# Seven quarter products for A11 B11 in the block pairs of six matrices, and another place for the last rows of one, in a relational graph layer on one core

## The chip, the core and the metric

The kernel runs on one core of a Trainium2 chip. The core has five engines with queues of their own: TensorE (matmuls, PE), VectorE (DVE), ScalarE (ACT), GpSimd (POOL) and SyncE (SP, which here only starts transfers). Each engine works through its queue in order, and engines wait for each other on semaphores. The metric is the device time of one launch in microseconds, lower is better. Given is the median of several executions, and besides one execution that was profiled.

## The reference, cut to what matters

```python
h = jnp.maximum(_layernorm(x, axis=-1), 0.0)          # x: 1250 x 1024
# u: root term, bias, and for 8 edge types the mean of the neighbours times a matrix
out = h @ root + bias
for r in range(8):
    mask = (edge_type == r).astype(h.dtype)
    sums = segment_sum(h[src] * mask[:, None], dst, num_segments=n)
    cnt = segment_sum(mask, dst, num_segments=n)
    out = out + (sums / jnp.maximum(cnt, 1.0)[:, None]) @ weight[r]
u = out
z = jnp.concatenate([u, h], axis=1) @ w_gate + b_gate
y = x + jnp.tanh(u) * z + h * (1.0 - z)
```

All is float32. There are 20000 edges, eight 1024 x 1024 matrices `weight[r]`, one `root`, and `w_gate` of 2048 x 1024.

## The kernel before, in words

The kernel multiplies first and gathers afterwards. It forms h times each matrix of the list `mats`: matrices zero to seven are `weight[0..7]`, eight is `root`, nine is the lower half of `w_gate` (for h), and ten is the upper half (for u). Products with the weights are stored to DRAM tables `y`. For each node GpSimd gathers the rows of `y` that belong to its incoming edges, and VectorE adds them to the node's row with a weight (L1170, here called a gather add). Gathers run beside the products of matrices five to nine. Matrix ten is the last stage, in which the gate is applied (L1496 on).

**Products of quarters.** The 1250 rows are ten blocks of 128. A step (s, i) takes matrix s with blocks i and i + 5 together, i from 0 to 4. The two row blocks and the matrix are cut into quarters (A11 to A22, B11 to B22; a B quarter is 512 x 512), and `product` (L341) forms the result with seven products in place of eight, by the Strassen-Winograd scheme. The sums of A quarters (S1 to S4) lie ready in `h_op[i]`; those of B quarters (t1 to t4) are made by VectorE for each matrix (`make_t1` to `make_t4`, L167 to L181). A product is four matmuls of 512 columns into one PSUM bank, and `product` runs them in the order A11 B11, S1 t1, S2 t2, then S4 B22, S3 t3, A12 B21 and A22 t4 (by the names of the code the first, fifth, sixth, third, seventh, second and fourth). TensorE adds up in PSUM; after some products ScalarE copies the bank out and VectorE adds other parts in SBUF. The bank `b` is a chain: A11 B11 is copied out as one result, then S2 t2 is added to the same bank, and so on.

**Pairs.** In matrices one to nine, steps 0 and 1, and steps 2 and 3, are pairs (`paired`, L446); step 4 stands alone. In a pair the product A12 B21 of both blocks is formed together, by seven smaller products over quarters of quarters (class `Second`, L183). From matrix four on (`thirds`, L450) S4 B22 is treated likewise (class `Third`, L254). Each small product is two matmuls of 256 columns (`Second.add`, L212), and needs sums that VectorE forms: `Second.right` and `left` (L201, L206), `Third.sums` and `next_sums` (L267, L273). Their tiles are the spare factor buffers `f.spare` and four tiles `room` (`inner0` to `inner3`). The pieces are slipped into the order of `product` by the dictionary `fill`, under the names of the products.

**What sets the order.** The program is scheduled by hand (`manual_schedule`, L54): each engine gets its instructions in the order in which the Python code emits them. After each product `done()` calls `between(j)`, j from 0 to 6; `step` uses it (`beside`, L477) to emit the loads of the next matrix, the sums for factors, and lastly one or two gather adds (`spread`, L1223). Where a sum of quarters is needed depends on TensorE's order, and where it stands in VectorE's queue on the `between` call that emitted it. In step 4 the factors of the next matrix are made (`make_t1` at j = 1, `make_t2` at 4, `make_t3` at 5), `make_t4` and the `right` and `left` sums at j = 0 of the next matrix's step 0.

**Memory.** Products take PSUM banks from `bank()`, six buffers named `ps`. Two more banks, `ps_n` and `ps_q`, hold the edge sorting's matmuls early on and two of `Third`'s sums later. A result row is a tile of the pool `rows` (four buffers, L102), stored by SP (`put`, L465).

Of the kernel before, what the change touches and what calls it, by code (L numbers as in the profile page):

```python
# [19 lines left out]
def tile_rgcn_highway(  # L20
# [98 lines left out]
    node_dram = [dram.tile([KEYS, 1], I32, name=f"node_dram{g}") for g in range(G)]  # L119

    def bank():
        return psum.tile([P, 512], F32, name="ps", bufs=6)


    wbuf = [wpool.tile([P, KQ, Q], F32, name=f"w{i}") for i in range(9)]
# [128 lines left out]
    class Third:  # L254
# [53 lines left out]
        def last_to(self, to, to1, c):  # L308
# [3 lines left out]
                                 to1.rearrange("p (a n) -> p a n", a=2),  # L312
                                 self.b[:, None, :].to_broadcast([P, 2, H]))

    def transposed(aop, part, of, n, relu=False):


        for half, to in enumerate(((A11, A12), (A21, A22))[part]):
            p = bank().rearrange("p (k f) -> p k f", k=KQ)
            for i in range(KQ):  # L320
                k = KQ * half + i
                nc.tensor.transpose(p[:, i, :n], of[:n, k * P:(k + 1) * P], ident[:n, :n])  # L322
            to_n, p_n = aop[:, to, :, :n], p[:, :, :n]
            if half and relu:
                nc.vector.tensor_scalar_max(to_n, p_n, 0.0)
            elif half:
                nc.vector.tensor_copy(to_n, p_n)
            else:
                nc.scalar.activation(to_n, p_n, AF.Relu if relu else AF.Copy)
            if n < P:  # L330
                nc.gpsimd.memset(aop[:, to, :, n:], 0.0)
# [7 lines left out]
                                                                     aop[:, b])  # L339

    def product(aop, w, to, between=lambda j: None, last=None, pieces=1, whole=True,  # L341
                fill=None, second=None, third=None, inner=None):

        c11, c12 = to[0][:, :Q], to[0][:, Q:]  # L350
        c21, c22 = to[1][:, :Q], to[1][:, Q:]
        step = [0]

        def add(b, i, fresh=False, at=slice(0, Q)):
            for k in range(KQ):
                nc.tensor.matmul(b[:, at], aop[:, i, k, :], w.of[i][:, k, at],  # L356
                                 start=(fresh and k == 0), stop=(k == KQ - 1),
                                 skip_group_check=True)

        def done():  # L360
            between(step[0])
            step[0] += 1

        def filled(name):
            if fill and name in fill and fill[name]():
                done()

        def p3():
            add(c, S4)
            if third:  # L370
                third(c)
            else:
                nc.vector.tensor_add(c12, c12, c)  # L373
            done()
            filled("third")

        def p7():
            d = rows.tile([P, Q], F32, name="part", bufs=2)
            add(b, S3)
            nc.scalar.copy(d, b)  # L380
            nc.vector.tensor_add(c22, c22, d)  # L381
            done()
            filled("seventh")
            return d

        def p2():
            a = bank()
            add(a, A12, True)
            nc.vector.tensor_add(c11, c11, a)
            done()  # L390

        b = bank()
        c = inner.hold() if inner and inner.holds else bank()
        add(b, A11, True)
        nc.scalar.copy(c11, b)  # L395
        done()
        filled("first")
        if second:
            second()
            p2()  # L400
        add(c, S1, True)
        nc.scalar.copy(c22, c)  # L402
        done()
        filled("fifth")
        add(b, S2)
        nc.scalar.copy(c12, b)  # L406
        done()
        filled("sixth")
        if whole and not third:
            p3()  # L410
            d = p7()
            if not second:
                p2()
        else:
            d = p7()
            if third:
                last(d, 0)
            if inner:
                inner.then(c)
                done()  # L420
                filled("third")
            else:
                p3()
        if pieces == 1:
            add(b, A22)
            if last:
                last(b, 0)
            else:
                nc.scalar.copy(c21, b)  # L429
        else:  # L430
            for j in reversed(range(pieces)):
                at = slice(j * Q // pieces, (j + 1) * Q // pieces)
                b = bank()
                add(b, A22, True, at)
                last(b[:, at], at.start, d[:, at])
        done()
        filled("fourth")
# [12 lines left out]
    def thirds(s):  # L450

        return s > EARLY

    waiting, waiting_third = {}, {}

    def step(s, i, between=lambda j: None, second=None):

        two = paired(s, i)
        t = [rows.tile([P, D], F32, name="row") for _ in range(2)]
        if two and i == 2:  # L460
            t.reverse()
        if two and i % 2 == 0:
# [12 lines left out]
            nc.sync.dma_start(to, t[:n])  # L475

        def beside(j):  # L477
            new = fac[s + 1]
            if i == 0 and j == 0 and s > 0:
                fac[s].make_t4()  # L480
            if two and i == 0:
                sums(j)
            if q and i % 2 == 0 and j == 1:
                q.sums()
            if q and i % 2 and j == 1:
                q.next_sums()
                q.first_to(to[:, Q:])
            if q and i % 2 and j == 4:
                q.fifth_to(t[0][:, Q:])
            if two and (i, j) == (1, 6):  # L490
                Second(fac[s], 2).left()
            if (s, i, j) == (0, 0, 3) or (s > 0 and (i, j) == (3, 0)):
                new.load_first()
            if (s, i, j) == (0, 0, 3) or (s > 0 and (i, j) == (3, 2)):
                new.load_next()
            if i == NP - 1:
                if j == 0:
                    new.load_b22()
                elif j == 1:
                    new.make_t1()  # L500
                elif j == 3:
                    new.load_b21()
                elif j == 4:
                    new.make_t2()
                elif j == 5:
                    new.make_t3()
            between(j)

        def sums(j):
# [5 lines left out]
            if j == (0 if s > EARLY else 4):  # L515
                e.left()

        fill = {}
        q = None
        if two:  # L520
            e, to = waiting[i - i % 2]
            if thirds(s):
                if i % 2 == 0:
                    waiting_third[i] = Third(fac[s], i, room)
                q = waiting_third[i - i % 2]
                q.holds = i % 2 == 0

                def then(c):
                    if q.holds:
                        q.second(c)  # L530
                    else:
                        q.last(c)
                        q.last_to(to[:, Q:], t[0][:, Q:], c)
                        put(i - 1, 0, to)

                q.then = then
            if i == 0:
                fill = dict(sixth=lambda: (e.second(), e.second_to_first(to)))
            elif i == 1:
                fill = dict(first=lambda: (e.first(), q and q.first(), 0)[-1],  # L540
                            fifth=lambda: (e.sixth(), True),
                            sixth=lambda: (e.seventh(), e.to_first(to), 0)[-1],
                            seventh=lambda: (e.fourth(), e.to_second(t[0]),
                                             q or put(i - 1, 0, to), 0)[-1],
                            third=lambda: (e.fourth_to_second(t[0]), 0)[-1])
            elif i == 2:
                fill = dict(sixth=lambda: e.first(),
                            seventh=lambda: e.sixth(),
                            third=lambda: (e.seventh(), e.to_first(to), 0)[-1],
                            fourth=lambda: (e.fourth(), True))  # L550
            else:
                fill = dict(first=lambda: (e.to_second(t[0]), e.fourth_to_second(t[0]),
                                           q and q.first(), 0)[-1],
                            sixth=lambda: (e.second(), True),
                            seventh=lambda: (e.second_to_first(to), q or put(i - 1, 0, to),
                                             0)[-1])
        product(h_op[i], fac[s], t, between=beside, whole=not two, fill=fill, second=second,
                inner=q)
        for part in range(2):
            if part or not two or i % 2:  # L560
                put(i, part, t[part])
# [578 lines left out]
    with ExitStack() as edges_part:  # L1140
# [4 lines left out]
        inner_pool = edges_part.enter_context(tc.tile_pool(name="inner", bufs=1))  # L1145
        room = [inner_pool.tile([P, 2, n], F32, name=f"inner{k}")
                for k, n in enumerate((H, H, P, P))]

        fresh = [GOT]

# [87 lines left out]
        def passes_needed():  # L1238
# [7 lines left out]
                                             w_of[:, g, d, K[g][d]:], axis=AX.X)  # L1246
            nc.vector.reduce_max(most[:, 1:2], far_k, axis=AX.X)
            for _ in range(30):
                yield
            p = bank()  # L1250
            nc.tensor.transpose(p[:1, :P], most[:, 0:1], ident)
# [327 lines left out]
```

## Time and profile before

| what | value |
|---|---|
| median of 3 runs | 1359.27 us (1354.49 to 1364.49) |
| the profiled execution | 1362.24 us |
| its span, first to last instruction | 1360.2 us |
| granted TensorE clock, mean | 0.996 |
| gather adds (L1170) | 193, 246.9 us on VectorE |
| matrix six (721 to 838 us): VectorE busy | 88.5 of 117 us |
| matrix nine (1079 to 1200 us): VectorE busy | 91.4 of 121 us |
| waits of gather adds for their gather | 86.3 us in 45 |

A group line of the profile reads: line, engine and operation, output<-inputs by the program's names, shapes, count | busy us, mean ns | idle time of the engine before it and what ended most of it. A timeline row reads: start, duration, engine, line, operation, count, and in brackets the idle time before it. An fp32 matmul of the program stands in the trace as two records. L numbers are lines of the kernel before.

### The profile page before, as it was taken

The numbers are of one execution on the slowest core, as the hardware profiler recorded it, in microseconds if no ns is written. First come the engines' busy times: TensorE is split into PE (matmuls) and PEld (weight loads), VectorE is DVE, ScalarE is ACT, GpSimd is POOL, SyncE is SP. The second block draws the span as 40 slices with busy tenths as digits, with TensorE's granted clock in tenths as the row PEclk, the third lists the DMA queues.
The fourth block names the chain that finished last, engine by engine and source line by source line (L and its number), as shares of the span: only waits on it lengthen the run. The fifth ranks groups of instructions, "written<-read, shape, count | busy, mean of one in ns | idle before, by whom it ended". The sixth has DMA issues, their size and how long they took to land.

```text
span 1360.2 us, 13211 instructions
## 1 busy us (share of the span) xinstructions
PE 1343.3 (99%) x3954; PEld 686.7 (50%) x3954; DVE 940.9 (69%) x1929; ACT 370.2 (27%) x816; POOL 583.6 (43%) x510
## 2 busy tenths in 40 slices
PE   9999999999999999999999999999999999989997
PEld 5444455455445545554554555455455455544443
DVE  6855967876785834425767777876867696667875
ACT  3335566465741111111111111111111111122210
POOL 0001655754552456001444564555366356434631
PEclk9999999999999999999999999999999999989999
DMA  8744675854863251144648779788788957879971
GB/s 307 273 184 151 93 141 139 212 85 110 175 167 108 54 156 34 46 155 151 213 126 303 236 240 357 255 284 290 240 274 281 315 178 227 284 263 270 337 202 58
DMA packets 106908, 271.15 MB, mean 199 GB/s; under 512 B 22692, under 2 KB 24946, under 8 KB 106704
## 3 DMA queue, kind: packets, MB, share of 16 engines
q1 hardware_dynamic: 46640, 120.01, 29.5%
q0 software_dynamic: 44064, 118.28, 27.8%
q10 hardware_dynamic: 16128, 31.98, 7.4%
q8 instruction: 31, 0.51, 0.2%
q14 instruction: 45, 0.37, 0.1%
HBM read 212.71 MB, written 75.66 MB: 212 GB/s over the span
## 4 chain that ended last, share of the span: by engine, by line
PE 76%; DMA 10%; issue 8%; POOL 4%; DVE 2%; SPq 0%; ACT 0%; POOLq 0%; DVEq 0%; ACTq 0%
PE ps L356 61%; PE ps L214 8%; DMA got<-y,idx 6%; PE ps_n L356 2%; PE ps_q L214 2%; DMA got<-hr_dram,node 2%; POOL got L1165 1%; PE ps_n L214 1%; DMA w<-in_L_gnn_weight_dram 1%; DVE u L1170 1%; DMA z_dram<-row 1%; POOL got L586 1%; POOL h_op L586 1%; PE ps L322 1%; POOL out_dram L592 1%
## 5 line engine op out<-in xcount | busy, mean ns | idle before, releaser
L356 PE MATMUL ps<-w,h_op 128*128 128x512 f32 x2512 | 1108.1, 594 | 5.4 <-ACT row L402 4.1
L356 PEld LDWEIGHTS ps<-w,h_op 128*128 128x128 f32 x2512 | 472.2, 190 | 548.2 <-issue 529.6
L1165 POOL DMA_INDIRECT got<-y,idx x193 | 247.3, 1281 | 345.3 <-DVE u L1170 212.1
L1170 DVE SCALAR_TENSOR_TENSOR u<-got,w_of,u 128x1024 f32<-128x1024 f32 (+1 forms) x193 | 246.9, 1282 | 88.8 <-DMA got<-y,idx 86.3
L982 POOL DMA_INDIRECT table<-row_col,at_i x157 | 176.5, 1124 | 157.4 <-DVE at_i L978 73.7
L381 DVE TENSOR_TENSOR row<-row,part 128x512 f32<-128x512 f32 x55 | 37.9, 689 | 113.9 <-ACT part L380 113.9
L429 ACT COPY row<-ps 128x512 f32<-128x512 f32 x50 | 29.2, 584 | 215.5 <-PE ps L356 215.5
L380 ACT COPY part<-ps 128x512 f32<-128x512 f32 x55 | 32.2, 585 | 180.4 <-PE ps L356 180.4
L395 ACT COPY row<-ps 128x512 f32<-128x512 f32 x55 | 32.2, 585 | 163.1 <-PE ps L356 157.9
L214 PE MATMUL ps<-w,w 128*128 128x256 f32 x288 | 71.3, 380 | 0.0
L406 ACT COPY row<-ps 128x512 f32<-128x512 f32 x55 | 32.2, 586 | 133.3 <-PE ps L356 133.3
L214 PEld LDWEIGHTS ps<-w,w 128*128 128x128 f32 x288 | 54.4, 190 | 18.3 <-issue 12.4
L402 ACT COPY row<-ps 128x512 f32<-128x512 f32 x43 | 25.1, 585 | 124.7 <-PE ps L356 108.1
L968 DVE SCALAR_TENSOR_TENSOR junk<-k_bc,key_col,before 128x128 f32<-128x128 int32 x157 | 55.0, 350 | 4.2
L908 DVE TENSOR_TENSOR seen<-seen,ps_n 128x100 f32<-128x100 f32 x157 | 40.2, 256 | 24.7 <-PE ps_n L903 20.6
L214 PE MATMUL ps<-w,h_op 128*128 128x256 f32 x216 | 56.0, 382 | 0.0
L373 DVE TENSOR_TENSOR row<-row,ps 128x512 f32<-128x512 f32 x30 | 20.5, 684 | 47.8 <-PE ps L356 32.2
L214 PEld LDWEIGHTS ps<-w,h_op 128*128 128x128 f32 x216 | 40.5, 190 | 25.6 <-issue 22.3
L169 DVE TENSOR_TENSOR w<-w,w 128x2048 f32<-128x2048 f32 (+1 forms) x12 | 25.3, 2112 | 37.1 <-PE ps L356 35.9
L885 ACT ACTIVATE is_lo<-io,less_lo 128x128 bf16<-128x128 f32 x157 | 50.2, 391 | 0.7 <-DMA xh_dram<-xt 0.7
L623 POOL DMA_INDIRECT node_dram<-ids,pos_i x20 | 28.8, 1440 | 41.5 <-issue 41.5
L356 PE MATMUL ps_n<-w,h_op 128*128 128x512 f32 x96 | 43.3, 593 | 1.6 <-DVE row L309 1.6
(216 smaller groups left out, 1180.8 us busy)
## 6 DMA issues: line engine op xcount, KB each, us to landing
y<-row SPq DMA_DIRECT2D x72, 512.0 KB
w<-in_L_gnn_weight_dram ACTq DMA_DIRECT2D x21, 1024.0 KB
w<-in_L_gnn_weight_dram SPq DMA_DIRECT2D x10, 1024.0 KB
k_bc<-keys_dram SPq DMA_DIRECT2D x39, 256.0 KB
l_bc<-los_dram SPq DMA_DIRECT2D x39, 256.0 KB
w<-in_L_gnn_w_gate_dram ACTq DMA_DIRECT2D x6, 1024.0 KB
h_dram<-h_op SPq DMA_DIRECT2D x9, 512.0 KB
u<-in_L_gnn_bias_dram SPq DMA_DIRECT2D x9, 512.0 KB
```

What stands on the lines that cost most here:

```text
L214: nc.tensor.matmul(p, a[:, k, :], b[:, k, :], start=(fresh and k == 0), stop=(k == 1), skip_group_check=True)
L356: nc.tensor.matmul(b[:, at], aop[:, i, k, :], w.of[i][:, k, at], start=(fresh and k == 0), stop=(k == KQ - 1), skip_group_check=True)
L380: nc.scalar.copy(d, b)
L381: nc.vector.tensor_add(c22, c22, d)
L395: nc.scalar.copy(c11, b)
L406: nc.scalar.copy(c12, b)
L885: nc.scalar.activation(is_lo[:, i, :], io, AF.Abs, bias=less_lo[:, c0 + i:c0 + i + 1])
L908: nc.vector.tensor_add(seen[j][:, i, :], was, p[:, i, :])
L968: nc.vector.scalar_tensor_tensor(junk, o["k_bc"][:, i, :], key_col[:, c:c + 1], before, op0=OP.is_equal, op1=OP.mult, accum_out=rank[:, c: ...
L982: ins = nc.gpsimd.indirect_dma_start(out=table[:, :], out_offset=bass.IndirectOffsetOnAxis(ap=at_i[:n, i:i + 1], axis=0), in_=row_col[:n, ...
L1165: nc.gpsimd.indirect_dma_start(out=t[:n], out_offset=None, in_=y[g][:, :], in_offset=bass.IndirectOffsetOnAxis(ap=at[:n, d, k:k + 1], axis=0),
L1170: nc.vector.scalar_tensor_tensor(u[:n], t[:n], w, u[:n], op0=OP.mult, op1=OP.add)
```

## The change

In matrices four to nine A11 B11 of both blocks of a pair takes seven products of quarters too. The class `First` does this. Unlike `Second` and `Third` it forms its results in PSUM alone: ScalarE or VectorE write a partial sum into a bank, and TensorE adds the next product on top. The two results, `to0` and `to1`, are then the banks `b` of the two blocks' chains. The first four small products (`early`) run one step ahead, before that step's last product; the last three (`late`) in the pair's first step, in which S1 t1 now comes first and the third product right after. `First` shares the tiles `room` with `Third`, has one more tile `p5_room`, and its banks are a name of their own, so `ps` has four buffers and `ps_b` two. `fill` and the positions j of some sums are rearranged for this, in odd steps the third product comes before the seventh, and in third blocks `seventh` and `fourth` of `Second` are emitted together. In matrix nine's step 4 the two result rows lie in the S2 and S3 places of `h_op[2]` and `h_op[3]`, not in row buffers. The transposes of `passes_needed` are emitted at j = 4 of a step 4.

```diff
     def bank():
-        return psum.tile([P, 512], F32, name="ps", bufs=6)
+        return psum.tile([P, 512], F32, name="ps", bufs=4)
+    def lead():
+        return psum.tile([P, 512], F32, name="ps_b", bufs=2)
...
+    class First:
+        def __init__(self, f, i, room, p5):
+            b = f.place["b11"]
...
+        def sums(self):
+            Third.sums(self)
+        def next_sums(self):
+            Third.next_sums(self)
+        def early(self):
+            self.to0 = lead()
+            self.x, y = bank()[:, :H], bank()[:, :H]
+            Second.add(self, self.x, self.a11, self.b11, True)
+            nc.scalar.copy(self.to0[:, :H], self.x)
+            Second.add(self, y, self.s1, self.t1, True)
+            nc.scalar.copy(self.p5, y)
+            Second.add(self, self.to0[:, :H], self.a12, self.b21)
+            Second.add(self, self.x, self.s2, self.t2)
+            nc.vector.tensor_add(self.to0[:, H:], self.x, self.p5)
+        def late(self):
+            self.to1 = lead()
+            Second.add(self, self.x, self.s1, self.t1)
+            nc.scalar.copy(self.to1[:, :H], self.x)
+            nc.vector.tensor_add(self.to1[:, H:], self.x, self.p5)
+            Second.add(self, self.to0[:, H:], self.s2, self.b22)
+            Second.add(self, self.to1[:, :H], self.a22, self.t2)
+            return self.to0
...
+        def p1():
+            if first is None:
+                b = lead()
+                add(b, A11, True)
+            else:
+                b = first.late() if inner.holds else first.to1
+            nc.scalar.copy(c11, b)
+            done()
...
+        if first and inner.holds:
+            c = p5()
+            b = p1()
+            inner.then(c)
+            done()
+        else:
+            b = p1()
...
         else:
+            if inner and not inner.holds:
+                inner.then(c)
+                done()
+                filled("third")
             d = p7()
             if third:
                 last(d, 0)
-            if inner:
-                inner.then(c)
-                done()
-                filled("third")
-            else:
+            if not inner:
                 p3()
+        if early:
+            early()
...
+    def next_first(s, i):
+        if thirds(s) and i == 1:
+            return s, 2
+        if thirds(s + 1) and i == NP - 1 and s + 1 < NM - 1:
+            return s + 1, 0
+        return None
...
-        t = [rows.tile([P, D], F32, name="row") for _ in range(2)]
+        if (s, i) == (NM - 2, NP - 1):
+            t = [h_op[k][:, S2:S3 + 1].rearrange("p a k f -> p (a k f)") for k in (2, 3)]
+        else:
+            t = [rows.tile([P, D], F32, name="row") for _ in range(2)]
...
-            if q and i % 2 == 0 and j == 1:
+            if q and i % 2 == 0 and j == 3:
                 q.sums()
...
-            if q and i % 2 and j == 4:
+            if q and i % 2 and j == 3:
                 q.fifth_to(t[0][:, Q:])
+            if coming and j == (4 if i == 1 else 2):
+                first_sums()
...
+        def first_sums():
+            waiting_first[coming] = First(fac[coming[0]], coming[1], room, p5_room)
+            waiting_first[coming].sums()
+        def early():
+            waiting_first[coming].early()
+            waiting_first[coming].next_sums()
...
             elif i == 2:
                 fill = dict(sixth=lambda: e.first(),
                             seventh=lambda: e.sixth(),
-                            third=lambda: (e.seventh(), e.to_first(to), 0)[-1],
                             fourth=lambda: (e.fourth(), True))
+                fill["fourth" if q else "third"] = lambda: (e.seventh(), e.to_first(to), 0)[-1]
+                if q:
+                    fill["fourth"] = lambda: (e.seventh(), e.to_first(to), e.fourth(), True)
...
             for _ in range(30):
                 yield
+            while at_call != [NP - 1, 4]:
+                yield
             p = bank()
```

## The prediction

> **What bounds the kernel now.** I read the busy times first, then what TensorE waits for, then the queue of VectorE around the places that the change touches.
>
> ```profile
> PE 1343.3 (99%) x3954; PEld 686.7 (50%) x3954; DVE 940.9 (69%) x1929; ACT 370.2 (27%) x816; POOL 583.6 (43%) x510
> ...
> PE ps L356 <- ACT row L402: 4.1, 1, 4.1
> PE ps_n L356 <- DVE row L309: 1.6, 1, 1.6
> ```
>
> TensorE is busy all the time, and its longest waits are one of 4.1 us and one of 1.6 us. So time is won only by fewer matmul columns or by those waits, and any new wait of TensorE is paid in full.
>
> ```profile
> 1201.30:1204.70 3.40, 0.44 (x2) 0.00 (x0) 2.16 (x1) 0.00 (x0) 2.67 (x2) 1.00 1.03 416
> 1204.70:1211.60 6.90, 5.78 (x7) 2.53 (x8) 0.00 (x0) 4.36 (x5) 0.00 (x0) 0.51 1.03 420
> ...
> 1205.18 0.58 ACT L402 COPY row<-ps 128x512 f32<-128x512 f32 x1 [9.64 <-DMA z_dram<-row]
> ```
>
> The windows (columns: stretch, sum, PE, PEld, DVE, ACT, POOL, then the granted clock) show the 4.1 us wait in matrix nine's last row block: a copy waits for a row buffer that is still being stored. The clock in the next 6.9 us is half. Work from 1205.8 to 1211.6 runs at half speed and loses another 2.9 us.
>
> ```profile
> 741.91 0.68 DVE L389 TENSOR_TENSOR row<-row,ps 128x512 f32<-128x512 f32 x1
> 742.51 2.28 DVE L177 TENSOR_TENSOR w<-w,w 128x2048 f32<-128x2048 f32 x1
> 744.72 2.60 DVE L1170 SCALAR_TENSOR_TENSOR u<-got,w_of,u 128x1024 f32<-128x1024 f32 x2
> 747.23 2.28 DVE L181 TENSOR_TENSOR w<-w,w 128x2048 f32<-128x2048 f32 x1
> ...
> 753.09 0.42 DVE L210 TENSOR_TENSOR w<-h_op,w 128x256 f32<-128x256 f32 x1
> 753.43 2.60 DVE L1170 SCALAR_TENSOR_TENSOR u<-got,w_of,u 128x1024 f32<-128x1024 f32 x2
> 755.94 0.42 DVE L268 TENSOR_TENSOR inner<-h_op 128x256 f32<-128x256 f32 x1
> ...
> 747.34 3.60 PE L356 MATMUL ps_n<-w,h_op 128*128 128x512 f32 x8
> ```
>
> This is VectorE's timeline from the last block of matrix five into the first of matrix six. Nothing between L389 and L268 has idle time before it: VectorE works off 14 us of queue in a row. L389 itself needs the product A12 B21, which ended at 740.48 (two products of 3.43 us before the ps_n product at 747.34). Today TensorE needs none of that queue soon.
>
> **Removed.** The trace shows an fp32 matmul as two records. Eight records of 512 columns take 3.43 us, start to next start, so 0.429 each; eight of 256 take 1.73, so 0.216:
>
> ```profile
> 802.59 3.60 PE L356 MATMUL ps<-w,h_op 128*128 128x512 f32 x8
> ...
> 806.02 1.89 PE L214 MATMUL ps<-w,w 128*128 128x256 f32 x8
> 807.75 1.03 PE L214 MATMUL ps_n<-w,h_op 128*128 128x256 f32 x4
> ```
>
> A pair's two A11 B11 are 16 records of 512, 6.86 us; the seven quarter products are 28 of 256, 6.05 us. Twelve pairs (matrices four to nine, two each): **-9.8**. Matrix nine's last rows go to old factors, so L402's wait and the slow clock behind it go: 4.1 + 2.9 = **-7.0**. The third product now comes before the seventh, 3.43 us earlier, so the 1.6 us on L309 goes: **-1.6**. Sum -18.4.
>
> **Added, first pairs.** In `late`, TensorE's a22 t4 into `to1[:, :H]` waits for VectorE's add into `to1[:, H:]` (same tile). In the changed program's order that add stands behind: the c11 add of A12 B21 (L389), make_t3 (L177), the gather adds, `early`'s add, four `next_sums`, make_t4 (L181), four `right` (L204), four `left` (L207 to L210) and the gather adds of the step: exactly the queue shown, plus 2.23 us (a quarter add 0.34 pace to pace, sums 1.88 as L268 to L271). TensorE arrives after `early` (16 records, 3.46), A22 (3.43), A11's place taken by S1 (3.43) and two quarter products (1.73): 12.05 us after A12 B21 ended. For matrix six: VectorE is through at 755.94 + 2.23 + 0.42 = 758.6; TensorE is there at 740.48 + 12.05 = 752.5: a wait of 6.1. The same sum from the other timelines, with VectorE's position after the last gather add of the queue (or the last L210) and the end of A12 B21 found as above:
>
> - matrix four: fourteen weight instructions (L609 to L615, 5.1 us) stand there in place of gather adds, and VectorE waits 0.6 for `early`: 520.20 + 2.23 + 0.6 + 0.42 against 505.87 + 12.05: 5.5
> - matrix five, no gathers: 632.30 + 3.25 against 623.06 + 12.05: 0.4
> - seven: 873.13 + 2.65 against 857.66 + 12.05: 6.1
> - eight, one gather add: 987.63 + 2.65 against 974.85 + 12.05: 3.4
> - nine: 1112.49 + 2.65 against 1092.04 + 12.05: 11.1. VectorE comes to L389 7.7 us late there, behind late gathers (5.9 us of waiting before 1088.8).
>
> Together **+32.6**. The first sums (1.9 us) put into the last block ahead of this are hidden: in matrices three to six VectorE waits 1.8 to 3.4 us for L381 after them, in seven and eight for gathers. Without that cover they would lengthen each of these waits by up to 1.9.
>
> **Added, second pairs.** The same wait stands at the third block. VectorE's queue there is shorter: from the third product's end, adds and first sums 3.4, two gather adds 2.6, L248 to L381 1.4, gather add 1.3, quarter adds and `next_sums` 2.6, `left` 1.4, two gather adds 2.6, 0.4: 15.8 us against TensorE's 16.3. Left is the handoff alone: copy and add behind the quarter product (0.62 + 0.5) less 0.86: 0.3 in five matrices. In matrix nine VectorE stands 7.4 us late at L309; I leave 5 of it, since the wait before lets it catch up. **+6.5** (2 to 12).
>
> **Added, third block.** `seventh` and `fourth` of Second now follow each other; the second needs ScalarE's copy of the first.
>
> ```profile
> 800.86 1.03 PE L214 MATMUL ps<-w,h_op 128*128 128x256 f32 x4
> ...
> 801.98 0.37 ACT L220 COPY w<-ps 128x256 f32<-128x256 f32 x1 [0.33 <-PE ps L214]
> ```
>
> TensorE could go on at 801.73, the copy ends at 802.35: 0.65 with the signal, six times: **+3.9** (0 to 4.5).
>
> **Added, the clock.** The row: 4.1 us of waiting halved the clock. Read alone, waits of 5.5, 6.1, 6.1 and 11.1 us all do it, four times 2.9, 11.6. [...]
>
> **At nothing.** 36 quarter copies of ScalarE (0.37 each, 13 us) lie in its 73% idle time; in the chain each is followed by a product of 0.86. VectorE's 120 new instructions (4.45 us a pair, 53 in all) beyond the waits above: it idles 28 of 117 us in matrix six (row below), but in nine it is full, which is a rival. PSUM's six banks become four and two: the banks taken in `early` were last read a product or more before. `sums` of Third moves two products later; L269 ends at 756.96 and is needed at 768.98, so cover remains. On SP the half-row store waits for the adds of one more product; behind it stand the next stores and `load_next`, not due for a block. If that cover were gone, a copy would wait as L402 did, 4 us. POOL issues the same.
>
> **Sum.** -18.4 + 32.6 + 6.5 + 3.9 + 9.3 = +33.9. The profiled run took 1362.2 (span 1360.2), 3 us over the median 1359.3. Carried to the median: **1393.2**.
>
> **Rivals.**
>
> ```profile
> 721.00:838.00 117.00, 117.00 (x329) 61.87 (x328) 88.50 (x105) 19.10 (x37) 59.02 (x50) 1.00 0.81 282
> 1079.00:1200.00 121.00, 118.91 (x332) 62.25 (x331) 91.39 (x108) 18.91 (x37) 66.10 (x50) 1.00 0.75 244
> ```
>
> *Faster:* VectorE reaches the add in `late` before TensorE does. For it: a quarter of VectorE's time is idle. The point is 12.05 us after A12 B21. Against: the queue starts only when that product ends, and takes 9.2 to 20.5 us before anything is added. Then -18.4 + 3.9 + 1.8 (the handoff at six second pairs): about 1347, and 1341 if the copies in the third block are covered too.
> *No change:* the waits come, but the clock stays up and matrix nine's falls to 5, VectorE having caught up: -18.4 + 26.5 + 3 + 3.9 = +15 at most, and a wait or two shorter brings it to 1365 to 1374.
> *Worse:* in matrix nine VectorE is busy 91 of 121 us and waits for gathers in most of the rest, so its 9 us of new work there and in eight isn't absorbed: 5 more at each pair of nine and 3 at the last products: about 1407.
> That the quarters don't replace the whole products is excluded by the program: 96 fewer matmuls of 512 columns, 168 more of 256.
>
> **Chances.** Forecast 0.70, worse 0.08, no change 0.13, faster 0.09. A change of less than about 1% (13.6 us) can't be told from none in this kernel: faster 0.06 (the faster rival's better part), same 0.17, slower 0.77. The unknown costs alone span 1372 to 1412; with part of the rivals on either side the range is 1364 to 1412.
>
> **What would show it.** Right: TensorE waits on VectorE's add in `late`, near 6 us in matrices four, six and seven, little in five, most in nine, and half clock after these; no L402 wait for z_dram; quarter products at 0.216 a record. Wrong: those waits under 2 us, or VectorE reaching `late` early.

## The result, and the profile after

| | before | after |
|---|---|---|
| median of 4 runs | 1356.93 us (1354.49 to 1364.49) | 1406.67 us (1403.78 to 1407.83) |
| the profiled execution | 1362.24 us | 1407.83 us |
| its span | 1360.2 us | 1406.0 us |
| granted TensorE clock, mean | 0.996 | 0.985 |

The ratio is 1.0349, with a 95% interval of 1.031 to 1.0388: slower. The time is 13.5 us above the forecast of 1393.2. Against the medians of this table the loss is 49.7 us, 15.8 more than the 33.9 forecast; the median of before is lower here than the 1359.27 the forecast started from, because a fourth run is in it.

Busy times come first again, from the page of the kernel after:

```profile
PE 1349.1 (96%) x4098; PEld 719.6 (51%) x4098; DVE 995.2 (71%) x2049; ACT 381.9 (27%) x852; POOL 589.3 (42%) x510
```

TensorE has 144 records more and is busy for 5.8 us longer, though it has less to do; the half clock of six stretches (37.6 us at 0.50 in all, TensorE busy in 24.4 of them) is in that number. The span grew by 45.8, so most of the loss is TensorE standing still. The waits of TensorE in the kernel after (engine, what it wrote, its line, what it waited for, the line of that; us in total, times, longest):

```profile
PE ps_b L218 <- DVE ps_b L354: 29.8, 7, 6.7
PE ps_b L400 <- ACT part L424: 8.1, 12, 0.7
PE ps L218 <- ACT w L235: 2.8, 6, 0.5
PE ps_q L1049 <- issue: 1.8, 1, 1.8
PE ps L366 <- DVE row L417: 1.5, 1, 1.5
```

L354 is VectorE's add in `late`, the wait that the forecast is built on. L235 is the copy in the third block, also forecast. The second line was not: L424 is ScalarE's copy of S3 t3 in `p7`. The waits on L402 and L309 of before are gone.

VectorE's timeline into matrix six, the counterpart of the one shown for before (start, duration, engine, line, operation, count):

```profile
759.02 0.67 DVE L433 TENSOR_TENSOR row<-row,ps 128x512 f32<-128x512 f32 x1
759.61 2.27 DVE L181 TENSOR_TENSOR w<-w,w 128x2048 f32<-128x2048 f32 x1
761.82 1.27 DVE L1266 SCALAR_TENSOR_TENSOR u<-got,w_of,u 128x1024 f32<-128x1024 f32 x1
763.01 0.41 DVE L348 TENSOR_TENSOR ps_b<-ps,inner 128x256 f32<-128x256 f32 x1
...
765.22 1.27 DVE L1266 SCALAR_TENSOR_TENSOR u<-got,w_of,u 128x1024 f32<-128x1024 f32 x1
766.41 2.27 DVE L185 TENSOR_TENSOR w<-w,w 128x2048 f32<-128x2048 f32 x1
768.62 0.67 DVE L208 TENSOR_TENSOR w<-w 128x512 f32<-128x512 f32 x1
...
772.26 0.42 DVE L214 TENSOR_TENSOR w<-h_op,w 128x256 f32<-128x256 f32 x1
772.60 2.60 DVE L1266 SCALAR_TENSOR_TENSOR u<-got,w_of,u 128x1024 f32<-128x1024 f32 x2
775.12 0.43 DVE L354 TENSOR_TENSOR ps_b<-ps,inner 128x256 f32<-128x256 f32 x1
```

From L433 (L389 before) to L354 VectorE is never idle: 16 us of queue. make_t4 (L185), the four `right` (L208) and four `left` (L211 to L214) take 766.41 to 772.60, 6.2 us, and nobody needs them before the add. TensorE's timeline over the same time, with the idle time before an instruction and its releaser in brackets, and one line of ScalarE's:

```profile
767.85 1.03 PE L218 MATMUL ps_b<-w,inner 128*128 128x256 f32 x4
775.60 2.07 PE L218 MATMUL ps_b<-inner,h_op 128*128 128x256 f32 x4 [6.72 <-DVE ps_b L354]
...
784.63 3.68 PE L400 MATMUL ps_b<-w,h_op 128*128 128x512 f32 x8
788.98 1.55 PE L400 MATMUL ps_b<-w,h_op 128*128 128x512 f32 x3 [0.68 <-ACT part L424]
```

```profile
788.34 0.59 ACT L424 COPY part<-ps_b 128x512 f32<-128x512 f32 x1 [3.79 <-PE ps_b L400]
```

The first wait is 6.72 us. At 784.63 begin the eight records of S3 t3; A22 t4 goes into the same bank and must wait until ScalarE has copied it out. It begins after 4.35 us in place of 3.43. By single records, from the start of the last one to the next start, less the usual 0.429, such a gap is 0.84 us; there are twelve, two in each of matrices four to nine.

The clock, in windows around that wait (stretch, sum, PE, PEld, DVE, ACT, POOL busy with counts, granted clock, DMA share, GB/s):

```profile
767.85:771.26 3.41, 1.03 (x5) 0.57 (x3) 3.38 (x6) 0.94 (x2) 3.10 (x2) 1.00 0.35 77
771.26:774.68 3.42, 0.00 (x0) 0.00 (x0) 3.35 (x6) 0.00 (x0) 0.76 (x2) 0.50 0.72 264
774.68:778.09 3.41, 2.49 (x6) 2.05 (x7) 3.38 (x5) 0.00 (x0) 2.80 (x3) 0.50 0.21 58
778.09:781.50 3.41, 3.41 (x7) 1.82 (x6) 3.04 (x5) 0.00 (x0) 1.91 (x3) 0.50 0.89 243
781.50:784.92 3.42, 3.42 (x11) 1.82 (x10) 0.03 (x1) 0.59 (x1) 2.04 (x3) 1.00 0.86 320
```

The clock falls to 0.50 while TensorE waits, and stays there for 5.9 us of work (2.49 + 3.41) after the wait has ended.

### The profile page after: what moved, and what is told of

Read it like the earlier page. It is cut to its first block, busy times and chain, and to the rows that moved or that the text cites. A ratio compares the mean times of both kernels' runs of the same rounds, so it can differ in the third digit from the quotient of the medians.

```text
span 1406.0 us, 13671 instructions
## 1 busy us (share of the span) xinstructions
PE 1349.1 (96%) x4098; PEld 719.6 (51%) x4098; DVE 995.2 (71%) x2049; ACT 381.9 (27%) x852; POOL 589.3 (42%) x510
## 5 line engine op out<-in xcount | busy, mean ns | idle before, releaser
L400 PE MATMUL ps_b<-w,h_op 128*128 128x512 f32 x1560 | 705.9, 598 | 9.1 <-ACT part L424 8.1
L400 PEld LDWEIGHTS ps_b<-w,h_op 128*128 128x128 f32 x1560 | 294.4, 191 | 344.1 <-issue 319.4
L1261 POOL DMA_INDIRECT got<-y,idx x193 | 260.7, 1351 | 373.6 <-DVE u L1266 231.5
L400 PE MATMUL ps<-w,h_op 128*128 128x512 f32 (+1 forms) x760 | 338.5, 589 | 0.0
L400 PEld LDWEIGHTS ps<-w,h_op 128*128 128x128 f32 x760 | 143.3, 190 | 163.4 <-issue 160.7
L424 ACT COPY part<-ps_b 128x512 f32<-128x512 f32 x55 | 32.2, 586 | 217.8 <-PE ps_b L400 215.8
L467 ACT COPY row<-ps_b 128x512 f32<-128x512 f32 x54 | 31.7, 586 | 202.3 <-PE ps_b L400 195.9
L492 ACT COPY row<-ps_b 128x512 f32<-128x512 f32 x49 | 28.7, 585 | 187.8 <-PE ps_b L400 186.4
L218 PE MATMUL ps<-w,h_op 128*128 128x256 f32 x264 | 69.0, 384 | 2.8 <-ACT w L235 2.8
L218 PEld LDWEIGHTS ps<-w,h_op 128*128 128x128 f32 x264 | 49.1, 190 | 31.7 <-issue 21.9
L442 ACT COPY row<-ps_b 128x512 f32<-128x512 f32 x54 | 31.7, 587 | 97.1 <-PE ps_b L400 82.6
L450 ACT COPY row<-ps 128x512 f32<-128x512 f32 x42 | 24.6, 586 | 109.3 <-PE ps L400 96.6
L218 PE MATMUL ps<-inner,inner 128*128 128x256 f32 x192 | 49.3, 379 | 0.0
```

The source lines that it names most:

```text
L218: nc.tensor.matmul(p, a[:, k, :], b[:, k, :], start=(fresh and k == 0), stop=(k == 1), skip_group_check=True)
L1261: nc.gpsimd.indirect_dma_start(out=t[:n], out_offset=None, in_=y[g][:, :], in_offset=bass.IndirectOffsetOnAxis(ap=at[:n, d, k:k + 1], axis=0),
```

## The experiments

Each experiment has a short name, given with its result. The ratios are to the kernel before, measured on the same chip in the same session; times from different sessions are compared through them. "The first wait" is that of a matrix's first pair on L354, as excess over the usual pace from start to start. In the kernel after it is 5.9, 0.6, 6.9, 6.3, 2.7 and 6.6 us in matrices four to nine, 28.9 in all.

**Theory A: the wait is the order of VectorE's queue. Rival: VectorE has too much work, in whatever order.** The edit moves what nobody needs yet behind the add:

```diff
-            if i == 0 and j == 0 and s > 0:
+            if i == 0 and s > 0 and j == (1 if s > EARLY else 0):
                 fac[s].make_t4()
...
-            for k in range(4) if s > EARLY and j == 0 else (j,) if s <= EARLY and j < 4 else ():
+            for k in range(4) if s > EARLY and j == 1 else (j,) if s <= EARLY and j < 4 else ():
                 e.right(k)
-            if j == (0 if s > EARLY else 4):
+            if j == (1 if s > EARLY else 4):
                 e.left()
```

> The changed kernel with make_t4 and the right and left sums of a step 0 emitted after its third call of done() position (j = 1) and no longer at j = 0, from matrix four on, so that VectorE's add in late stands ahead of them. Theory A (the wait is the order of VectorE's queue): these instructions are 2.25 + 8 x 0.5 = 6.3 us of the queue ahead of the add. TensorE's excess at the first pair falls from 5.9, 0.6, 6.9, 6.3, 2.7 and 6.6 us to 0.3 to 0.7 each, 28.9 to about 3.6 in all, and the half clock behind them (10.7 us of excess) goes: 1406.7 - 25 - 10.7 = about 1371 us. Rival B (VectorE has too much work beside matrices six to nine, whatever its order): the waits move to the sums that were put back (L211 to L214, L218 on w) or to L354 in the second pair; 1395 or more.

Measured (both_moved): 1376.52 us, ratio 1.0097 (1.0066 to 1.0129). Its longest waits:

```profile
PE ps_b L400 <- ACT part L424: 8.1, 12, 0.7
PE ps_b L218 <- DVE ps_b L354: 7.5, 5, 2.5
PE ps_q L1049 <- ACT s_b L1033: 3.6, 2, 2.3
PE ps L366 <- DVE row L417: 3.3, 1, 3.3
PE ps L218 <- ACT w L235: 2.8, 6, 0.5
```

and VectorE at the same place of matrix six:

```profile
757.56 3.91 DVE L1266 SCALAR_TENSOR_TENSOR u<-got,w_of,u 128x1024 f32<-128x1024 f32 x3
761.39 0.42 DVE L354 TENSOR_TENSOR ps_b<-ps,inner 128x256 f32<-128x256 f32 x1
761.72 2.28 DVE L185 TENSOR_TENSOR w<-w,w 128x2048 f32<-128x2048 f32 x1
```

Where L185 stood in front of L354 it now stands behind it, and the first waits are 0.8 in six, 1.5 in nine and under 0.3 elsewhere. The mean granted clock of both_moved's profiled execution is 0.997, against 0.985 in the kernel after. A good 2.5% of the time, some 34 of the 49.7 us, is this order with the half clock behind it. Not all is: the *second* pairs of six, eight and nine now wait 1.7, 1.7 and 2.7 us on L354, where VectorE runs through 20 to 26 us of queue without a gap. So the rival holds in part, for these. Each of those three queues begins with a gather add that had waited 1.0 to 5.1 us for its gather, so late gathers may have a part in it. The one of six:

```profile
786.20 1.28 DVE L1266 SCALAR_TENSOR_TENSOR u<-got,w_of,u 128x1024 f32<-128x1024 f32 x1 [5.11 <-DMA got<-y,idx]
```

The dose: `right` and `left` moved alone, make_t4 left where it was.

> The changed kernel with only the eight right and left sums emitted at j = 1 in place of j = 0; make_t4 stays ahead of the add in late. Theory A (queue order): each first wait that is longer than that falls by the 8 x 0.5 = 4.05 us taken from the queue: matrix four 5.9 to 1.9, six 6.9 to 2.8, seven 6.3 to 2.2, nine 6.6 to 2.6, five and eight to 0.3 to 0.7; about 10.5 us in all in place of 28.9. The clock: stalls of 2 to 3 us are under the shortest one that halved it so far (2.7 us, in eight), so it mostly stays up: 1406.7 - 18.4 - 7 to 10.7 = 1378 to 1381 us. Rival B (VectorE full): waits of 5 us and more remain in six to nine, 1395 or more.

Measured (sums_moved): 1381.13 us, ratio 1.0145 (1.0101 to 1.0188).

```profile
PE ps_b L218 <- DVE ps_b L354: 13.1, 6, 3.9
```

The first waits were 1.7, under 0.3, 2.9, 2.3, under 0.3 and 4.0: four, six and seven lost 4.0 to 4.2 us each, as much as was taken from the queue. Nine lost less (2.6 for 4.05), probably since TensorE had saved time in the matrices before it and VectorE hadn't.

The other way to shorten the queue is to leave its order and make its gather adds short:

```diff
-            nc.vector.scalar_tensor_tensor(u[:n], t[:n], w, u[:n], op0=OP.mult, op1=OP.add)
+            nc.vector.scalar_tensor_tensor(u[:n, :P], t[:n, :P], w, u[:n, :P], op0=OP.mult,
+                                           op1=OP.add)
```

> The changed kernel with each gather add on 128 of its 1024 columns; the rest of the gathered rows is left out of the sums, all transfers stay. Theory A (the wait in late is the length of VectorE's queue): each gather add falls from 1.28 to about 0.3 us; five stand in the queue ahead of the add in six and seven (6.9 to about 2, 6.3 to about 1.4), eight and nine fall to 0.3 to 0.7, four and five, with no gather adds, stay at 5.9 and 0.6. About 11 us of first waits in place of 28.9, the second pairs at 0.3 each, half clock left behind matrix four alone: 1406.7 - 18 - 1.7 - 8 = about 1379 us. Rival (VectorE's late point is set by when the gathers land, not by its own work): waits in six, seven and nine stay at 5 us and more, above 1395.

Measured (short_gathers): 1382.2 us, ratio 1.0171 (1.0131 to 1.021).

```profile
PE ps_b L218 <- DVE ps_b L354: 13.1, 6, 5.7
...
1002.25 0.27 DVE L1507 TENSOR_SCALAR piece_at<-node 128x1 int32<-128x1 int32 x3 [1.65 <-DVEq L1410]
```

First waits 5.9, 0.6, 2.2, 1.6, 2.5, 1.3. Matrices four and five, which have no gather adds there, are unchanged; six, seven and nine fall by about 5. Eight hardly falls, where 0.3 to 0.7 was expected: ahead of its add VectorE idles 1.65 us at a branch of the program (L1410), which no count of the queue had in it. In six, seven and nine the wait is the length of what stands ahead of the add, not the landing of gathers: VectorE stands as long in front of late gathers as in the kernel after (40 us against 38 between 735 and 1240 us).

**Theory C: the twelve gaps on L424 are a cost of their own.** In even steps the third product goes back to its place between S3 t3 and A22 t4; in step 3 another product is put there:

```diff
             b = p1()
-            inner.then(c)
-            done()
...
             if third:
                 last(d, 0)
+            if inner and inner.holds:
+                inner.then(c)
+                done()
...
+                if q:
+                    fill["sixth"] = lambda: False
+                    fill["third"] = lambda: False
+                    fill["seventh"] = lambda: (e.second(), e.second_to_first(to),
+                                               put(i - 1, 0, to), True)
```

> The changed kernel with a product put between S3 t3 and A22 t4 again, on another bank: in even steps the third product is emitted there (as before the change), and in step 3 its stand-in, second of Second with second_to_first. Theory C (a term that the forecast left out: A22 t4 goes into the bank that ScalarE must first copy out for S3 t3, L424, and 12 times nothing lies between): the 12 gaps of 0.84 us go, the rest stays: 1406.7 - 10.1 = about 1396.6 us. Rival (the 0.84 us are only a part of a wait that is due anyway, since VectorE's queue is the limit, so that TensorE waits as much longer at the next L354): the waits on L354 grow by 0.84 each, 1403 to 1407.

Measured (cover): 1408.76 us, ratio 1.034 (1.0295 to 1.0385), the same as the change. Its waits:

```profile
PE ps_b L218 <- DVE ps_b L354: 37.5, 7, 9.0
PE ps_q L218 <- DVE inner L279: 4.3, 4, 1.5
PE ps L218 <- DVE inner L279: 3.4, 2, 2.0
```

No L424 is left, so the gaps were what they seemed, and in matrices four and five, where VectorE keeps up, the gain is kept: from the end of the first wait in four to the beginning of that in six took 239.6 us in the kernel after and 236.7 here (four gaps are 3.4). From matrix six on it is given back: L354 costs 7.7 us more, unevenly (the first waits of seven, eight and nine grow by 2.9, 3.4 and 1.5), and L279 costs 7.7 that were not there. Of these, 4.3 (on `ps_q`) are a sum for the third product of step 3, which now comes a small product earlier, and 3.4 (on `ps`) a sum for `late`, which the edit doesn't move. The rival is right about the total, and about the kind of loss, not about its even spread.

**Theory D: the handoff in the third block.**

```diff
                 if q:
-                    fill["fourth"] = lambda: (e.seventh(), e.to_first(to), e.fourth(), True)
+                    fill["seventh"] = lambda: (e.sixth(), e.seventh(), 0)[-1]
+                    fill["fourth"] = lambda: (e.to_first(to), e.fourth(), True)
```

> The changed kernel with seventh of Second emitted together with sixth, one product ahead of fourth, in the third blocks of matrices four to nine. Theory D (the handoff to ScalarE's copy L235 costs 0.63 us each time): six waits of 0.63 us go: 1406.7 - 3.8 = about 1402.9 us. Rival (sixth and seventh then follow each other on banks that wait for each other, or the late add is reached earlier and waited for longer): 1405 to 1408.

Measured (seven): 1401.31 us, ratio 1.0289 (1.0246 to 1.0332). The six waits on L235 are gone. The ratio is 0.6% lower where 0.3% was expected, but its interval overlaps that of the kernel after, so the size of the gain is not shown. The first wait of matrix nine rose from 6.6 to 8.0.

**Do the terms add?** All three edits together, and the first and third without the second:

> The changed kernel with three edits together: make_t4, right and left at j = 1, a product again between S3 t3 and A22 t4, and seventh of Second with sixth. If the terms simply add: against the kernel before +13 us (the first edit alone) - 10.1 - 3.8, so the same time as before, ratio 0.999. If VectorE's amount of work is the limit from matrix six on, as the grown waits of the run cover hint (matrices seven to nine took 7.8 us more at L354 there): what TensorE saves in matrices six to nine comes back as waits on L354, L279 and L214, and only four and five keep theirs (a third: -4.6): ratio 1.004 to 1.008.

> The changed kernel with make_t4, right and left at j = 1, and seventh of Second with sixth; S3 t3 and A22 t4 stay neighbours. Terms add: +13 - 3.8 = 9 us over the kernel before, ratio 1.007. VectorE's amount of work as the limit: six to nine give their 0.63 us back in the second pair's wait on L354, ratio 1.009.

Measured: 1380.14 us, ratio 1.0148 (1.0103 to 1.0192) for all three (all3), and 1369.73 us, 1.0084 (1.0056 to 1.0111) for two (both_seven). Both my expectations of all3 were too low: the edit that was to win 10 us lost between 8 and 9. Waits of all3:

```profile
PE ps_b L218 <- DVE ps_b L354: 9.9, 5, 3.0
PE ps_q L218 <- DVE inner L279: 7.4, 4, 3.1
PE ps L218 <- DVE inner L273: 6.6, 3, 3.8
PE ps L218 <- DVE inner L279: 2.2, 2, 1.4
```

These are 26.1 us. In both_seven L354 took 7.5, L273 0.9, L279 0.3 and L424 8.1, together 16.8. The 9.3 between them, with 5.2 us of half clock that only all3 has (its mean granted clock is 0.995, that of both_seven 0.998), are about the 14.2 us between the two profiled executions; the ratios differ by 8.7 us. The waits on L273 are sums for `early`, those on L279 sums for the third product of step 3 (`ps_q`) and for `late` (`ps`). With the gaps gone TensorE comes to all these places before VectorE has the sums ready. both_seven's result doesn't separate its two expectations.

Is it VectorE's work in all3, or the gathers that it waits for? all3 with short gather adds, and the same cut in the kernel before as a control:

> all3 with each gather add on 128 of its 1024 columns (the rest of the gathered rows is left out of the sums; all transfers stay). If VectorE's own work is what makes TensorE wait in six to nine of all3 (about 26 us of waits on L354, L279 and L273): they go, and about 1380 - 24 = 1356 us. If VectorE stands behind gathers that land late (it idled 74 us for them in matrices six to nine of all3, 39 in the changed kernel): most of the waits stay, 1370 us or more.

> The kernel before with each gather add on 128 of its 1024 columns (the rest of the gathered rows is left out of the sums, all transfers stay): the control to all3_short. In the kernel before TensorE waits for VectorE in one place (1.6 us at L309), so a lighter VectorE brings at most that: ratio 0.998 to 1.000, and all3_short's 0.9949 is then the change's own gain with VectorE out of the way. Rival (the shorter gather adds by themselves speed up something else, such as the copy that waits for a row buffer or the last stage): ratio 0.995 or less, and all3_short's gain is not the change's.

Measured: 1350.36 us, ratio 0.9949 (0.9927 to 0.9971), for all3 with short gather adds (all3_short), and 1354.48 us, 0.9973 (0.996 to 0.9986), for the control (short_before). The longest waits of all3_short:

```profile
PE ps L366 <- DVE row L417: 2.0, 1, 2.0
PE ps L366 <- DVE h_op L796: 1.8, 1, 1.8
```

All waits on L354, L279 and L273 are gone, though every gather is still transferred and VectorE stands even longer in front of late ones (99 us between 735 and 1240 us, against 69 in all3): it was VectorE's work. The control says how to read the rest. The kernel before gains 0.3% by short gather adds too, so of the 0.5% only about 0.24% (some 3 us) would be the change's own, and the two intervals overlap. Even with VectorE out of the way these seven products were not shown to be worth anything. The profile of all3_short says where 6.9 of their 9.9 us went: 3.2 on the twelve handoffs at L354, 0.27 each, 2.0 on the wait for L417, in the last stage, and 1.7 on the half clock behind it (mean granted clock 0.997, in the control 0.998). The control has none of the three.

**The last rows alone**, put into the kernel before:

```diff
-        t = [rows.tile([P, D], F32, name="row") for _ in range(2)]
+        if (s, i) == (NM - 2, NP - 1):
+            t = [h_op[k][:, S2:S3 + 1].rearrange("p a k f -> p (a k f)") for k in (2, 3)]
+        else:
+            t = [rows.tile([P, D], F32, name="row") for _ in range(2)]
```

> The kernel before with one part of the change alone: the last two result rows of matrix nine lie in the S2 and S3 places of h_op[2] and h_op[3], as in the changed kernel. The copy's 4.1 us wait for a row buffer and the 2.9 us of half clock behind it go: -7.0, ratio 0.995. Rival (the copy then meets another wait, or the stores behind it end the kernel as late as before): ratio 0.998 to 1.001.

Measured (rows_only): 1355.78 us, ratio 0.9977 (0.9962 to 0.9991). The wait of 4.1 us has become

```profile
PE ps L356 <- ACT row L402: 0.3, 1, 0.3
```

and no half clock follows (mean granted clock 0.999), yet the median falls by 3.1 us (1.2 to 5.2), not by 7.0. The profiled execution of before was 5.3 us above its median, so it may have caught a long instance of that wait; how long it is in executions without a profile can't be seen. This version is the only one, with the reference's whole result, that beats both kernels.

**The class where it costs least.** In both_moved matrices four and five had no waits on L354, so `First` was kept there alone, in all3 (cut to the lines added to its three edits):

```diff
-        if thirds(s) and i == 1:
+        if EARLY < s < EARLY + 3 and i == 1:
             return s, 2
-        if thirds(s + 1) and i == NP - 1 and s + 1 < NM - 1:
+        if EARLY < s + 1 < EARLY + 3 and i == NP - 1:
             return s + 1, 0
```

> The three edits of all3, and class First in matrices four and five alone, where VectorE was ahead of TensorE at late in both_moved and all3; in six to nine A11 B11 is formed whole again. Four pairs at 6.86 - 6.05 = 0.82 us each give -3.3, last rows of matrix nine -3.1 (the median of rows_only), the wait on L309 up to -1.6; with the handoffs covered nothing is added: -6 to -8 us, ratio 0.994 to 0.9955. Rival (two PSUM banks fewer for the rest, or VectorE's queue in six to nine, cost by themselves): waits of TensorE in six to nine remain and the ratio is 1.0 or more.

Measured (four_five): 1358.06 us, ratio 1.0004 (0.9986 to 1.0021). Missed: no wait on VectorE is left in matrices four to nine. But four gaps on L424 (2.7 us) are, one in each of matrices six to nine: without `First` nothing of `early` stands there between S3 t3 and A22 t4. And there is this, in the last stage:

```profile
PE ps L366 <- DVE row L417: 4.6, 1, 4.6
```

```profile
1259.33 1.23 DVE L1488 TENSOR_TENSOR u<-u,got 128x1024 f32<-128x1024 f32 x1 [2.19 <-DMA got<-hr_dram,node]
```

VectorE has just waited for the gathered h times `root`, and L417 stands behind that. In this profile what TensorE had saved in the products it spent at the next place where it needs VectorE.

## Why the forecast had the right sign and was 13.5 us short

The two profiled executions side by side, by the terms of the sum (us; waits found as excess over the usual pace from start to start, which is 0.1 to 0.2 more than the idle time in the profile's rows):

| term of the forecast | forecast | found |
|---|---|---|
| quarter products for whole ones | -9.8 | -9.9 |
| last rows of matrix nine, with clock | -7.0 | -7.2 |
| L309 | -1.6 | -1.7 |
| first pairs | +32.6 | +28.9 |
| second pairs | +6.5 | +3.3 |
| third block | +3.9 | +3.8 |
| clock behind these waits | +9.3 | +10.7 |
| copy of S3 t3 (L424), not in the sum | 0 | +10.1 |
| before matrix four, not in the sum | 0 | +5.3 |
| last stage (L417), not in the sum | 0 | +1.5 |
| sum | +33.9 | +44.8 |

The spans differ by 45.8; 1.0 is in small gaps not listed. The medians differ by 49.7, which is 3.9 more; that the last rows gave 7.2 in the profile and 3.1 in the median of rows_only is about as large. There was luck in the total: the pairs were forecast 6.9 too dear, and that hid part of what was left out.

- *The step that failed* is the first sentence on the third product: "The third product now comes before the seventh, 3.43 us earlier, so the 1.6 us on L309 goes". I counted what the moved product reaches sooner, and not the place that it leaves. It had stood between S3 t3 and A22 t4, which share a bank with a copy between them, and had covered that copy. Twelve times 0.84 is 10.1 us, the largest term that the sum lacks. It is a cost in the account of this kernel and not 10.1 us to be had: in cover the gaps went and the time stayed. The same handoff was seen and priced at the third block, where it bore on two quarter products.
- *First pairs.* The queue, read from before and followed by hand, gave 5.5, 0.4, 6.1, 6.1, 3.4 and 11.1; found were 5.9, 0.6, 6.9, 6.3, 2.7 and 6.6. That the cause is the order is shown by both_moved, sums_moved and short_gathers. Nine was too large: I took VectorE as 7.7 us late there, as it was in before. In the kernel after it begins that add (L433) at 1137.94, 3.4 us after the end of A12 B21 at 1134.58: TensorE's waits in six, seven and eight had let it catch up. In the run seven, where TensorE loses less on the way, nine's wait is 8.0.
- *Second pairs.* 0.3 in five matrices was right to the tenth; nine waited 2.0 and not 5, for the same reason.
- *The clock.* The row of before alone would have given 11.6. No run shows the 9.3 that stands in the sum; the kernel after showed 10.7. Four waits were counted, and it was five: behind the wait of 2.7 us in matrix eight (2.54 of idle time in the profile) the clock was 0.50 for 3.41 us as well. The last section has what was measured.
- *Before matrix four*, +5.3 in the profiled execution, of which 1.65 is half clock (0.50 from 249.0 to 252.4 us). The kernel after reached the first wait of matrix four at 522.96 us. The eight experiments with `First` throughout have the same order of TensorE's work up to there; seven of them reached that place at 517.2 to 519.7 us, and both_moved at 523.3. So some 4 us of it vary between executions and are not the change.
- *The rivals.* "Worse" named 1407 (its terms add up to 1406), which is where the time fell, but by matrix nine being saturated, and nine's waits were smaller than forecast. The number was right by luck and the mechanism wrong. "Faster" fell in the kernel as it is, and came nearest to true in all3_short.
- *At nothing.* VectorE's idle time was called a cover beyond the waits priced. In the kernel as changed that held; with TensorE quicker (cover, all3) it did not. Much of that idle time stands in front of gather adds that wait for their gather (between 735 and 1240 us, 80 us in the kernel before and 70 in all3), and work queued behind them can't use it. ScalarE's quarter copies cost nothing outside the handoffs named. What the split of PSUM's banks into four and two costs was not tried by itself; four_five keeps it and ends with the time of the kernel before.

## What to carry to other kernels

When a product is moved, ask two things: what it now waits for, and what it had been covering where it stood. Seven quarter products won 0.82 us a pair here, and one uncovered handoff from TensorE over ScalarE's copy (L424) to TensorE cost 0.84, so such a change lives or dies by the order of the queues and not by the columns saved. And an add that TensorE waits for is to be emitted ahead of everything on its engine that is needed later: moving three calls by one position was worth 34 us here.

## What the runs showed of the clock

In the kernel after, the wait in matrix eight and the work behind it (columns as above):

```profile
1023.85:1027.26 3.41, 0.87 (x4) 0.67 (x4) 3.38 (x9) 0.59 (x1) 0.76 (x1) 1.00 0.01 2
1027.26:1030.67 3.41, 3.41 (x8) 2.33 (x8) 1.18 (x3) 0.00 (x0) 2.49 (x4) 0.50 0.62 178
```

Three pairs of neighbouring stretches of other runs; first sums_moved:

```profile
879.18:882.59 3.41, 1.30 (x7) 1.08 (x7) 3.34 (x6) 0.59 (x1) 2.61 (x5) 1.00 0.93 327
882.59:886.00 3.41, 3.41 (x7) 1.97 (x6) 3.38 (x8) 0.00 (x0) 0.92 (x1) 0.50 0.96 353
```

all3:

```profile
874.83:878.24 3.41, 1.42 (x6) 1.07 (x7) 3.38 (x4) 0.00 (x0) 2.91 (x4) 1.00 0.85 261
878.24:881.66 3.42, 3.42 (x6) 1.35 (x5) 3.38 (x6) 0.00 (x0) 2.61 (x2) 0.50 0.76 252
```

both_moved:

```profile
1277.15:1280.57 3.42, 1.48 (x13) 1.23 (x11) 1.33 (x2) 1.20 (x2) 2.61 (x2) 1.00 1.03 405
1280.57:1283.98 3.41, 2.02 (x8) 1.26 (x9) 3.34 (x6) 0.00 (x0) 2.10 (x2) 1.00 1.03 423
```

In the kernel after, 2.54 us of idle time (3.41 less 0.87 busy) are followed by a stretch at 0.50. So are 2.11 us in sums_moved (3.41 less 1.30) and 2.0 in all3 (3.41 less 1.42, rounded); 1.94 in both_moved (3.42 less 1.48) are followed by one at 1.00. These are single instances, and what decides between them was not shown. The clock of the kernel after was at 0.50 from 771.26 to 781.50 us, so the 6.7 us of waiting in matrix six were followed by 5.9 us of slow work.
